# Attention and perception in one kernel: key tile 0 of half groups 5 and 15 as three one-pass products, sums by transfer for 15 of 16 half groups, and small VectorE operations joined or moved

## The chip, the cores and the metric

The kernel runs on one core of a Trainium2 chip. The metric is the device time of one launch in microseconds. A core has five engines that run their own instruction streams side by side: TensorE (PE in the profile; PEld is its weight load), VectorE (DVE), ScalarE (ACT), GpSimd (POOL) and SyncE (SP). Transfers between HBM and SBUF are started by SP, ACT and POOL.

## What is computed

Input x has 4 images of 64x64 pixels with 256 channels, all in float32. Layer 0 is full self-attention within each image, layer 1 a 3x3 depthwise "perception", a two-layer update and local attention over a 3x3 window:

```python
q, k, v = x @ Wq, x @ Wk, x @ Wv             # 32, 32 and 256 channels; 4096 pixels an image
x = gamma * softmax(q @ k.T) @ v + x
perceived = depthwise_conv3x3(x)             # 256 -> 768 channels
h = x + w_up2 @ gelu(w_up1 @ perceived)      # 768 -> 512 -> 256
q, k, v = split(h @ w_qkv)                   # 256 channels each
w = softmax over the 9 neighbours of (q . k) / 16
out = h + sum over the 9 neighbours of w * v
```

## The kernel before

**Slots and points.** The work goes through 32 slots (NSLOT); a slot is 512 queries (8 rows) of one image, eight slots make an image. Within a slot the image's 4096 keys are taken in 16 half groups, n = 0 to 15, of 256 keys, that is two key tiles of 128. A loop over 16 "points" per slot writes the instruction order by hand: each engine executes its instructions in the order in which this loop gives them. At point n stand, in this order: load_alone for half group n+1, loads of keys and values of later groups, the high parts for n+1, the energy (scores and Exp) of half group n+2, send for n+1, jobs of layer 1, product n, add_up for n+1, and some perception taps. Layer 1 follows at a distance: perception two slots behind, the hidden layer three (k = slot - 3), the local result five (a = slot - 5). A slot of attention with layer 1 beside it takes about 92.6 us.

**The product, plain and in parts.** p, the exponentials of a half group, is a 128 x 2 x 512 tile. A plain product (L481) multiplies each key tile's values (128 keys, 256 channels in two halves) with its 512 columns of p, in float32 for which TensorE makes several passes; the trace has two records for each. In parts, p is cut into high (p rounded down to the one-pass type fp32r, by ScalarE, L428 and L437), low = p - high, and gap = high - 4096 * low (VectorE, L446 and L447 for one key tile, L510 and L520 for two). Three one-pass products per channel half then stand in place of a plain one: high by v and low by a form of v go to acc banks 0 and 1, gap by another form to banks 2 and 3; evacuate joins them at the slot's end. Even half groups but 0 have both tiles in parts (IN_PARTS). Odd ones have key tile 1 in parts in "full" slots (ONE_IN_PARTS), and half groups 11 and 13 key tile 0 too (BOTH_IN_PARTS). Full slots are those with 0 < s < 31 and s > 2 that are not the last of an image: 25 of 32. alone(s, n) names the tiles that are cut one by one, load_alone loads their value forms (vo, from packed_o), high_alone and low_and_gap make the three parts. For key tile 0 of half groups 11 and 13 all four tiles stand in the "hid" buffer, which is free in the second half of a slot.

**The sums.** The softmax denominator needs the sum of p over the half groups. Those in by_dma are added by accumulating transfers that POOL issues (send, L498 and L500), even ones into one tile and odd ones into another (tags "xc" and "sent"); the rest VectorE adds (L513, L516). At n = 15 VectorE adds the two sent tiles (L528), folds (L529), and partial_sums transposes and reduces (L547, L548). A small matmul (dps, L576) and reciprocal follow in the next slot, where finish scales the result into the ring of rows xp. In full slots half groups 0 to 13 go by transfer, in the first slot of an image from 2 on; 14 and 15 are VectorE's.

**Layer 1 pieces that the change touches.** border_terms (L992, L993) forms the border pixels' key sums: one ScalarE multiply for channel half 0, one VectorE multiply-add for half 1, into edge; border then sums edge over the partitions by one matmul (L1004). local_values adds the bias to each half of a PSUM bank on VectorE (L1033). scores multiplies the local exponentials by a mask on POOL (L1086); for the first slot of an image POOL also clears rows of them (L1093, L1095). local_sum adds the pieces up on POOL (L1109, L1112, L1115). local_product scales the local result on VectorE (L1167), adds h (L1179) and has SP send it to HBM (L1180), one channel half at point 4 and one at point 5; its tiles come from the tag "o", which has two buffers and also holds the results of evacuate.

**Buffers.** tile_of(shape, tag, name, bufs) takes the next of a tag's buffers; an instruction that writes into a buffer waits until what used it before is done, a transfer's landing included. "den" has one buffer: the sum, and then the inverse of the denominator, until finish is through.

Of the kernel before, what the change touches and what calls it, by code (L numbers as in the profile page):

```python
# [9 lines left out]
F32 = mybir.dt.float32  # L10
F32R = mybir.dt.float32r
AF = mybir.ActivationFunctionType
ALU = mybir.AluOpType
AX = mybir.AxisListType
PSUM = bass.MemoryType.PSUM

P = 128
B, H, W, C = 4, 64, 64, 256
N = H * W
CQK = C // 8  # L20
CH = C // P
HP, WP = H + 2, W + 2
NB = 512
RB = NB // W
WARM = 10
NBLK = N // NB
# [10 lines left out]
NHC = HID // P  # L37
# [5 lines left out]
NSLOT = B * NBLK  # L43
# [7 lines left out]
BELOW = 1.0 - 2.0**-13  # L51
IN_PARTS = (2, 4, 6, 8, 10, 12, 14)
ONE_IN_PARTS = (1, 3, 5, 7, 9, 11, 13, 15)
BOTH_IN_PARTS = (11, 13)
BY_DMA = (3, 5, 7, 9, 11, 13)
BY_DMA_IF_FULL = tuple(range(14))


LAG_PERC, LAG_HID, LAG_ATT = 2, 3, 5
# [3 lines left out]
def attention_then_perception_kernel(  # L63
# [19 lines left out]
    nc = tc.nc  # L83
# [8 lines left out]
    ones = const.tile([P, P], F32, tag="ones", name="ones")  # L92
# [8 lines left out]
    def unshifted():  # L101
        fctx = ExitStack()
        pool = fctx.enter_context(tc.tile_pool(name="fast", bufs=1))
# [4 lines left out]
        def tile_of(shape, tag, name, bufs=1):  # L108
            return pool.tile(shape, F32, tag=tag, name=name, bufs=bufs)
# [37 lines left out]
        for r in range(4):  # L147
            nc.scalar.dma_start(
                out=bqk2[r * CQK : (r + 1) * CQK, :], in_=b_qk[:, r % 2 : r % 2 + 1]
# [17 lines left out]
        for r in range(KR):  # L167
            m = near[r * KW : (r + 1) * KW]
            for half in range(2):

                for sign in (1, -1):
                    nc.gpsimd.affine_select(
                        out=m[:, half], in_=m[:, half], compare_op=ALU.is_ge, fill=0.0,
# [20 lines left out]
        def watch(values):  # L194

            n = values.free_size()
            for i in range(0, n, P):
                at = watched[:, : min(P, n - i)]
                nc.gpsimd.tensor_tensor(at, at, values[:, i : min(n, i + P)], ALU.add)
# [22 lines left out]
        def full(s):  # L222
            return in_two_sums(s) and s > 1 and s % NBLK < NBLK - 1
# [3 lines left out]

        def alone(s, n):

            return [i for i, ns in enumerate((BOTH_IN_PARTS, ONE_IN_PARTS)) if full(s) and n in ns]  # L230

        def load_parts(to, s, which):
            pair, r = divmod(s, 2)
# [74 lines left out]
        def load_values(s, G):  # L308
            values[s, G] = tile_of([P, TPB, C], "v", f"v_{s}_{G}", 2)
            to = values[s, G].rearrange("p t c -> p (t c)")  # L310
            at = block(s, G)
            if not in_two_sums(s):
                nc.sync.dma_start(out=to, in_=packed_v[:, bass.ts(at, TPB * C)])
            elif full(s):
                nc.sync.dma_start(out=to, in_=packed_h[:, at])
            else:
                nc.sync.dma_start(out=to[:, : 2 * C], in_=packed_h[:, at, : 2 * C])
                nc.sync.dma_start(out=to[:, 2 * C :], in_=packed_v[:, bass.ts(2 * at + 1, 2 * C)])
# [8 lines left out]
        def load_alone(s, n):  # L327
            for i in alone(s, n):
                if i:
                    f, *rest = [tile_of([P, NB], "vs", f"vo_{s}_{n}", 4)] + [None] * 3  # L330
                else:
                    four = tile_of([P, NHC, NB], "hid", f"vo_{s}_{n}_0")
                    f, *rest = (four[:, j] for j in range(NHC))
                forms[s, n, i], rests[s, n, i] = f, rest
                nc.sync.dma_start(
                    out=f.rearrange("p (f c) -> p f c", c=C), in_=packed_o[:, block(s, n // 2), i]
                )
# [71 lines left out]
        sums, accs, lsums, lrdens = {}, {}, {}, {}  # L409
# [92 lines left out]
        def add_up(s, G, half):  # L502

            n = 2 * G + half
            low_and_gap(s, n)
            p = weights[s, G, half]
            if in_parts(s, G, half):
                high = highs[s, G, half]
                low, gap = (tile_of([P, 2, NB], f"p{x}", f"p{x}_{s}_{G}_{half}") for x in "lg")
                nc.vector.tensor_tensor(low.bitcast(F32R), p, high, ALU.subtract)  # L510
            if not by_dma(s, n):
                if s in sums:
                    nc.vector.tensor_tensor(sums[s], sums[s], p, ALU.add)  # L513
                elif s in firsts:
                    sums[s] = tile_of([P, 2, NB], "den", f"den_{s}")
                    nc.vector.tensor_tensor(sums[s], firsts.pop(s), p, ALU.add)  # L516
                else:
                    firsts[s] = p
            if in_parts(s, G, half):
                nc.vector.scalar_tensor_tensor(  # L520
                    gap.bitcast(F32R), low, -SPLIT, high, ALU.mult, ALU.add
                )
                lows[s, G, half], gaps[s, G, half] = low, gap
            if G == NG - 1 and half == 1:
                den = sums[s]
                for even in range(2):
                    if (s, even) in sent:
                        nc.vector.tensor_tensor(den, den, sent.pop((s, even)), ALU.add)  # L528
                nc.vector.tensor_tensor(den[:, 0, :], den[:, 0, :], den[:, 1, :], ALU.add)  # L529

        def squares(t):
            return t.rearrange("p (j r) -> p j r", r=SQ)
# [6 lines left out]
        def partial_sums(s):  # L539


            a = shared(s)
            parts_[s] = tile_of([P, 2, NJ], "parts", f"parts_{s}")
            turneds[s] = tile_of([P, CH, NB], "xc", f"turned_{s}", 2)
            todo = [sums[s][:, 0, :]] + ([] if a is None else [lsums.pop(a)])
            for i, t in enumerate(todo):
                nc.vector.transpose(turneds[s][:, i, :], t)  # L547
                nc.vector.tensor_reduce(  # L548
                    parts_[s][:, i, :], squares(turneds[s][:, i, :]), axis=AX.X, op=ALU.add
                )  # L550
            watch(parts_[s][:, : len(todo), :].rearrange("p i j -> p (i j)"))

        def on_all(values, turned, out, copy=nc.vector.tensor_copy):

# [82 lines left out]
        def late_tile(name):  # L637

            if not thirds:
                t = perc_tile(name).rearrange("p s n -> p (s n)")  # L640
                thirds[:] = [t[:, i * NB : (i + 1) * NB] for i in range(3)]
            return thirds.pop(0)
# [323 lines left out]
        def edge_row(s):  # L966
            return {0: 0, NBLK - 1: RB - 1}.get(s % NBLK)

        edge = pool.tile([P, 2 * RB + W], F32, tag="edge", name="edge")

        def border_parts(s):

# [15 lines left out]
        def border_terms(s):  # L988


            for to, of in border_parts(s):
                nc.scalar.mul(edge[:, to], of(0), wc[:, 0:1])  # L992
                nc.vector.scalar_tensor_tensor(  # L993
                    edge[:, to], of(1), wc[:, 1:2], edge[:, to], ALU.mult, ALU.add
                )

        def border(s):


            ps = job_bank(f"c_{s}")  # L1000
            row = edge_row(s)
            n_side = 2 * RB
            n = border_parts(s)[-1][0].stop
            nc.tensor.matmul(ps[0:1, :n], lhsT=ones[:, 0:1], rhs=edge[:, :n], start=True, stop=True)  # L1004
            one = pad[0:1, :]
            nc.scalar.activation(one[:, :n], ps[0:1, :n], AF.Exp, bias=bc, scale=-(C**-0.5))
            nc.gpsimd.tensor_scalar(one[:, :n], one[:, :n], 3.0, None, ALU.mult)
            if row is not None:

                ends = one[:, n_side : n : W - 1]  # L1010
                nc.gpsimd.tensor_scalar(ends, ends, 2.0 / 3.0, None, ALU.mult)
# [4 lines left out]
        def local_values(s, t):  # L1016
            ps = job_bank(f"lv_{s}_{t}")
            for half in range(2):
                for kin in range(CH):
                    nc.tensor.matmul(  # L1020
                        ps[:, half * C : (half + 1) * C],
                        lhsT=keys_of(s, t, half, kin), rhs=wlv[:, kin, :],
                        start=(kin == 0), stop=(kin == CH - 1),
                    )
            for half in range(2):
                if s < NSLOT - 2:
                    lvs[s, t, half] = tile_of([P, C], "lv", f"lv_{s}_{t}_{half}", 8)
                else:
                    if not half:
                        late[s, t] = late_tile(f"lv_{s}_{t}")  # L1030
                    lvs[s, t, half] = late[s, t][:, half * C : (half + 1) * C]
                lv = lvs[s, t, half]
                nc.vector.tensor_tensor(lv, ps[:, half * C : (half + 1) * C], blv, ALU.add)  # L1033
                if s >= NSLOT - 1:

                    square = tile_of([P, 2, NB], "den", f"lv_{s}_{t}_{half}_2")[:, 0, :C]
                    nc.gpsimd.tensor_tensor(square, lv, lv, ALU.mult)
                    watch(square)

        def pieces(s):  # L1040

# [9 lines left out]
        def scores(s, half):  # L1051
# [31 lines left out]
            mask = near[:, half, :rows, :].rearrange("p h w -> p (h w)")  # L1083
            mask = mask.unsqueeze(1).to_broadcast([P, tiles, rows * QW])
            if s < NSLOT - 2:
                nc.gpsimd.tensor_tensor(pv, pv, mask, ALU.mult)  # L1086
            else:
                nc.vector.scalar_tensor_tensor(
                    pv, pv, 1.0, mask, ALU.mult, ALU.mult, accum_out=seen()
                )  # L1090
# [735 lines left out]
```

## Time and profile before

| what | value |
|---|---|
| median of 3 runs | 3201.46 us (3201.24 to 3201.75) |
| the profiled execution's own time | 3203.15 us |
| its span, first to last instruction | 3201.4 us |
| granted TensorE clock | 0.998 |
| busy PE / DVE / ACT / POOL | 3179.4 / 2903.6 / 1550.8 / 759.6 us |
| moved by transfers | 683.26 MB, mean 213 GB/s |
| sent<-p, 512 KB, issue to landing | 6.5 us (median of 356) |
| out<-lo, 256 KB, issue to landing | 3.9 us (median of 56) |

The page gives busy time by engine, the span in 40 slices, the transfers, the chain of work that ended last, and groups of instructions with count, busy time and mean duration. The timeline lists instructions in order of time: start in us, length in us, engine, line, operation, output<-inputs, shape, count, and in brackets the idle time before it and what ended it. The windows give busy time of PE, PEld, DVE, ACT and POOL in a stretch, then clock, transfer share and GB/s. Matmul ends are modelled, so steps between starts are used for TensorE.

### The profile page before, as it was taken

The page shows a single profiled execution, that of the slowest core. Times are in us where ns is not written, and L with a number is a line of the kernel's source. Part 1 is how long each engine was busy: PE and PEld are TensorE (multiplying, and loading weights), DVE is VectorE, ACT ScalarE, POOL GpSimd, SP SyncE. Part 2 cuts the span into 40 slices and gives each one's busy share as a digit, 9 for nine tenths or more (in the row PEclk, how much of TensorE's full clock was granted, in tenths as well). Part 3 has the DMA queues.
Part 4 walks back from the last instruction along what each step waited for, and adds up shares of the span by engine and source line. Part 5 has one row for each costly group of instructions (what it writes and reads, how often), then busy time and mean ns, then how long its engine had stood idle before and what let it go on. Part 6 is the DMA issues. An engine that isn't in the chain of part 4 may idle for free.

```text
span 3201.4 us, 39239 instructions
## 1 busy us (share of the span) xinstructions
PE 3179.4 (99%) x12486; PEld 2261.7 (71%) x12486; DVE 2903.6 (91%) x4428; ACT 1550.8 (48%) x2068; POOL 759.6 (24%) x1055
## 2 busy tenths in 40 slices
PE   9999999999999999999999999999999999999998
PEld 5557777766777777776777777777677777777655
DVE  5778999998999999998999999998899999999894
ACT  4435555445545555544555545554555555455331
POOL 3201122212222221222122232211221222222121
PEclk9999999999999999999999999999999999999999
DMA  7768888777888888877878888886788888888100
GB/s 259 229 170 218 227 226 224 220 230 229 227 227 243 243 218 229 221 208 247 234 219 232 225 240 234 238 221 197 269 238 221 224 228 227 235 237 220 50 25 28
DMA packets 315588, 683.26 MB, mean 213 GB/s; under 512 B 100384, under 2 KB 101424, under 8 KB 315248
## 3 DMA queue, kind: packets, MB, share of 16 engines
q1 hardware_dynamic: 243008, 435.69, 42.6%
q0 software_dynamic: 64688, 231.54, 31.7%
q10 hardware_dynamic: 7680, 13.44, 1.1%
q8 instruction: 104, 1.70, 0.2%
q14 instruction: 108, 0.88, 0.1%
HBM read 412.46 MB, written 80.61 MB: 154 GB/s over the span
## 4 chain that ended last, share of the span: by engine, by line
PE 94%; DVE 3%; DMA 1%; issue 0%; POOL 0%; ACT 0%; SPq 0%; ACTq 0%; DVEq 0%; POOLq 0%
PE acc L481 46%; PE e L418 7%; PE dx L857 7%; PE hid_de L800 5%; PE hid_gf L800 5%; PE hid_bc L800 5%; PE lv L1020 3%; PE g L953 3%; PE lo L1154 3%; PE v L347 3%; PE s L1061 2%; PE hid_a L800 2%; DVE perc L687 1%; PE qk L272 1%; PE hid L832 1%; DMA vo<-packed_o 0%
## 5 line engine op out<-in xcount | busy, mean ns | idle before, releaser
L687 DVE SCALAR_TENSOR_TENSOR perc<-xp,wb,perc 128x526 f32<-128x526 f32 (+1 forms) x1356 | 937.7, 757 | 0.4
L423 ACT ACTIVATE p<-e 128x1024 f32<-128x1024 f32 x512 | 524.9, 1025 | 485.9 <-PE e L418 409.4
L481 PE MATMUL acc<-p,v 128*128 128x512 f32 x1472 | 678.9, 596 | 0.2 <-ACT v L363 0.2
L500 POOL DMA_DIRECT2D sent<-p x304 | 258.0, 855 | 1353.6 <-ACT p L423 823.0
L481 PEld LDWEIGHTS acc<-p,v 128*128 128x128 f32 x1472 | 275.1, 190 | 267.9 <-issue 257.6
L418 PE MATMUL e<-qa,ka 128*128 128x512 f32 x1024 | 357.1, 430 | 5.3 <-ACT p L423 1.5
L428 ACT ACTIVATE ph<-p 128x1024 fp32r<-128x1024 f32 x203 | 215.1, 1060 | 198.4 <-PE acc L481 134.7
L510 DVE TENSOR_TENSOR pl<-p,ph 128x1024 fp32r<-128x1024 f32 x203 | 256.1, 1262 | 16.8 <-ACT ph L428 16.8
L481 PE MATMUL acc<-ph,v 128*128 128x512 f32 x812 | 264.3, 447 | 0.2
L520 DVE SCALAR_TENSOR_TENSOR pg<-pl,ph 128x1024 fp32r<-128x1024 f32 x203 | 253.3, 1248 | 11.9 <-DVE pl L510 0.5
L418 PEld LDWEIGHTS e<-qa,ka 128*128 128x128 f32 x1024 | 190.9, 188 | 86.0 <-issue 39.9
L437 ACT ACTIVATE oh<-p 128x512 fp32r<-128x512 f32 x200 | 126.4, 632 | 248.4 <-PE acc L481 83.2
L857 PE MATMUL dx<-hid,wup 128*128 128x512 f32 x512 | 229.8, 592 | 0.0
L481 PE MATMUL acc<-pl,vf 128*128 128x512 f32 x812 | 223.3, 397 | 0.0
L481 PE MATMUL acc<-pg,vf 128*128 128x512 f32 x812 | 219.1, 391 | 2.0 <-DVE pg L520 2.0
L481 PEld LDWEIGHTS acc<-ph,v 128*128 128x128 f32 x812 | 148.2, 189 | 51.9 <-issue 26.8
L481 PE MATMUL acc<-oh,v 128*128 128x512 f32 x400 | 184.8, 543 | 0.0
L481 PEld LDWEIGHTS acc<-pg,vf 128*128 128x128 f32 x812 | 152.3, 188 | 39.1 <-DVE pg L520 3.3
L481 PEld LDWEIGHTS acc<-pl,vf 128*128 128x128 f32 x812 | 152.7, 188 | 37.1
L823 ACT ACTIVATE hid<-hid,bup 128x512 f32<-128x512 f32 x120 | 80.3, 716 | 199.1 <-DVE hid L807 199.1
L693 DVE TENSOR_TENSOR perc<-perc 128x262 f32<-128x262 f32 x360 | 170.8, 488 | 6.3
L857 PEld LDWEIGHTS dx<-hid,wup 128*128 128x128 f32 x512 | 96.7, 189 | 98.5 <-issue 93.4
(231 smaller groups left out, 5476.1 us busy)
## 6 DMA issues: line engine op xcount, KB each, us to landing
sent<-p POOLq DMA_DIRECT2D x356, 512.0 KB, 6.5
vf<-packed_f SPq DMA_DIRECT2D x203, 512.0 KB, 5.7
v<-packed_h SPq DMA_DIRECT2D x200, 512.0 KB, 4.7
ka<-packed SPq DMA_DIRECT2D x1016, 64.0 KB, 3.3
vo<-packed_o SPq DMA_DIRECT2D x250, 256.0 KB, 3.9
xp<-in_x SPq DMA_DIRECT2D x30, 528.0 KB, 6.9
packed_f<-vlg POOLq DMA_DIRECT2D x28, 512.0 KB, 4.3
xc<-in_x SPq DMA_DIRECT2D x56, 256.0 KB, 4.3
```

The lines of the kernel that those rows point to most:

```text
L418: nc.tensor.matmul(e[:, i, :], lhsT=keys[s, G][:, bass.ts(2 * half + i, P)].bitcast(F32R), rhs=queries[s].bitcast(F32R), start=True, stop= ...
L423: nc.scalar.activation(p, e, AF.Exp)
L428: nc.scalar.activation(high.bitcast(F32R), weights[s, G, half], AF.Identity, scale=BELOW)
L437: nc.scalar.activation(high.bitcast(F32R), p, AF.Identity, scale=BELOW)
L481: nc.tensor.matmul(accs[s][to + c], lhsT=w[:, bass.ts(c, P)].bitcast(kind), rhs=x.bitcast(kind), start=to not in started[s], stop=last,)
L500: nc.gpsimd.dma_start(out=sent[s, even], in_=p, accum_op=ALU.add)
L510: nc.vector.tensor_tensor(low.bitcast(F32R), p, high, ALU.subtract)
L520: nc.vector.scalar_tensor_tensor(gap.bitcast(F32R), low, -SPLIT, high, ALU.mult, ALU.add)
L687: nc.vector.scalar_tensor_tensor(acc, win, wt, acc, ALU.mult, ALU.add)
L693: nc.vector.tensor_tensor(t[:, to, :], t[:, a, :], t[:, b, :], op)
L800: nc.tensor.matmul(ps[:, n * C : (n + 1) * C], lhsT=w(j), rhs=rows_of(mixes[s, j][:, kind, :]), start=(j == 0), stop=(j == MULT - 1),)
L857: nc.tensor.matmul(ps, lhsT=wup2[:, d, bass.ts(c, P)], rhs=hids[s][:, d, :], start=(d == 0), stop=(d == NHC - 1),)
```

## The change

Key tile 0 of half groups 5 and 15 joins the tiles in parts (5 not in the first slot of an image, where v's plain tile is loaded over the high one). For 15 its four tiles stand in "hid", as for 11 and 13; for 5 the value form and the high part stand in "den", low and gap in the two buffers of "o". Half group 14 is summed by transfer too, so only 15 is left to VectorE, which starts the sum from the even sent tile. partial_sums reduces both transposed tiles in one operation. The border's second channel half is multiplied on ScalarE and added by a second matmul. local_values adds the bias in one operation of 512 columns. The masks go from POOL to VectorE.

```diff
-BOTH_IN_PARTS = (11, 13)
+BOTH_IN_PARTS = (5, 11, 13, 15)
-BY_DMA_IF_FULL = tuple(range(14))
+BY_DMA_IF_FULL = tuple(range(15))
...
         def alone(s, n):
-            return [i for i, ns in enumerate((BOTH_IN_PARTS, ONE_IN_PARTS)) if full(s) and n in ns]
+            if not full(s) or n not in ONE_IN_PARTS:
+                return []
+            return [0, 1] if n in BOTH_IN_PARTS and (n > NHC * 2 or s % NBLK) else [1]
...
                 nc.sync.dma_start(out=to, in_=packed_h[:, at])
+                n = 2 * G + 1
+                if n in BOTH_IN_PARTS and 0 not in alone(s, n):
+                    nc.sync.dma_start(
+                        out=to[:, 2 * C : 3 * C],
+                        in_=packed_v[:, (2 * at + 1) * 2 * C : (2 * at + 1) * 2 * C + C],
+                    )
...
                     f, *rest = [tile_of([P, NB], "vs", f"vo_{s}_{n}", 4)] + [None] * 3
-                else:
+                elif n > NHC * 2:
                     four = tile_of([P, NHC, NB], "hid", f"vo_{s}_{n}_0")
                     f, *rest = (four[:, j] for j in range(NHC))
+                else:
+                    two = tile_of([P, 2, NB], "den", f"vo_{s}_{n}_0")
+                    f, *rest = two[:, 0], two[:, 1], *(
+                        tile_of([P, NB], "o", f"o{x}_{s}_{n}_0", 2) for x in "lg"
+                    )
...
                     nc.vector.tensor_tensor(sums[s], sums[s], p, ALU.add)
-                elif s in firsts:
+                elif n == 0:
+                    firsts[s] = p
+                else:
+                    first = firsts.pop(s) if s in firsts else sent.pop((s, 1))
                     sums[s] = tile_of([P, 2, NB], "den", f"den_{s}")
-                    nc.vector.tensor_tensor(sums[s], firsts.pop(s), p, ALU.add)
-                else:
-                    firsts[s] = p
+                    nc.vector.tensor_tensor(sums[s], first, p, ALU.add)
...
             for i, t in enumerate(todo):
                 nc.vector.transpose(turneds[s][:, i, :], t)
-                nc.vector.tensor_reduce(
-                    parts_[s][:, i, :], squares(turneds[s][:, i, :]), axis=AX.X, op=ALU.add
-                )
-            watch(parts_[s][:, : len(todo), :].rearrange("p i j -> p (i j)"))
+            parts = parts_[s][:, : len(todo), :].rearrange("p i j -> p (i j)")
+            turned = turneds[s][:, : len(todo), :].rearrange("p i n -> p (i n)")
+            nc.vector.tensor_reduce(parts, squares(turned), axis=AX.X, op=ALU.add)
+            watch(parts)
...
             for to, of in border_parts(s):
-                nc.scalar.mul(edge[:, to], of(0), wc[:, 0:1])
-                nc.vector.scalar_tensor_tensor(
-                    edge[:, to], of(1), wc[:, 1:2], edge[:, to], ALU.mult, ALU.add
-                )
+                for c in range(CH):
+                    nc.scalar.mul(edge[:, c, to], of(c), wc[:, c : c + 1])
...
-            nc.tensor.matmul(ps[0:1, :n], lhsT=ones[:, 0:1], rhs=edge[:, :n], start=True, stop=True)
+            for c in range(CH):
+                nc.tensor.matmul(
+                    ps[0:1, :n], lhsT=ones[:, 0:1], rhs=edge[:, c, :n],
+                    start=(c == 0), stop=(c == CH - 1),
+                )
...
-                nc.vector.tensor_tensor(lv, ps[:, half * C : (half + 1) * C], blv, ALU.add)
...
+            bias = blv.unsqueeze(1).to_broadcast([P, 2, C])
+            nc.vector.tensor_tensor(lv, ps.rearrange("p (a c) -> p a c", a=2), bias, ALU.add)
...
             if s < NSLOT - 2:
-                nc.gpsimd.tensor_tensor(pv, pv, mask, ALU.mult)
+                nc.vector.tensor_tensor(pv, pv, mask, ALU.mult)
```

The value projection splits a block's key tile 0 as well for the two half groups (the branch "both" of project_v), eight blocks in all.

More of the change, by code (lines that the diff above doesn't have):

```diff
@@ L967, in edge_row @@
             return {0: 0, NBLK - 1: RB - 1}.get(s % NBLK)
-        edge = pool.tile([P, 2 * RB + W], F32, tag="edge", name="edge")
+        edge = pool.tile([P, CH, 2 * RB + W], F32, tag="edge", name="edge")
         def border_parts(s):
@@ L1024, in local_values @@
                     )
+            if s < NSLOT - 2:
+                lv = tile_of([P, 2, C], "lv", f"lv_{s}_{t}", 4)
+            else:
+                lv = late_tile(f"lv_{s}_{t}").rearrange("p (a c) -> p a c", a=2)
             for half in range(2):
[L1026 to L1032, printed above, removed]
-                nc.vector.tensor_tensor(lv, ps[:, half * C : (half + 1) * C], blv, ALU.add)
[L1034 to L1038, printed above, removed]
+                lvs[s, t, half] = lv[:, half]
+            bias = blv.unsqueeze(1).to_broadcast([P, 2, C])
+            nc.vector.tensor_tensor(lv, ps.rearrange("p (a c) -> p a c", a=2), bias, ALU.add)
+            if s >= NSLOT - 1:
+                square = tile_of([P, 2, NB], "den", f"lv_{s}_{t}_2")[:, 0, :]
+                nc.gpsimd.tensor_tensor(square.rearrange("p (a c) -> p a c", a=2), lv, lv, ALU.mult)
+                watch(square)
         def pieces(s):
```

## The prediction

> **What bounds the kernel now.** I read the page first, then busy time in stretches of 100 us, then one slot (1018 to 1110 us, slot 11) as VectorE's timeline, TensorE's chain of waits and SyncE's transfers.
>
> ```profile
> PE 3179.4 (99%) x12486; PEld 2261.7 (71%) x12486; DVE 2903.6 (91%) x4428; ACT 1550.8 (48%) x2068; POOL 759.6 (24%) x1055
> ...
> PE 94%; DVE 3%; DMA 1%; issue 0%; POOL 0%; ACT 0%; SPq 0%; ACTq 0%; DVEq 0%; POOLq 0%
> ```
>
> TensorE (PE) is never without work, so only fewer passes on it make the kernel shorter. But VectorE (DVE) is full beside it wherever attention and perception run together:
>
> ```profile
> 1000.00:1100.00 100.00, 100.00 (x412) 74.82 (x411) 96.08 (x144) 52.65 (x70) 27.02 (x33) 1.00 0.86 235
> 1100.00:1200.00 100.00, 100.00 (x410) 74.35 (x409) 96.22 (x140) 50.34 (x65) 31.67 (x40) 1.00 0.84 229
> ```
>
> The third busy number is DVE's: 96%, and most of the rest is a few hundredths between instructions. In slot 11, 92.8 us long, its idle pieces over 0.1 us add up to 2.1 us, 1.6 of them just after the slot's start. So there are two clocks, and a delay of DVE of over some 2 us in one place reaches TensorE. The place that matters is half group 5, where a local result is written out:
>
> ```profile
> 1054.96 0.69 DVE L1167 SCALAR_TENSOR_TENSOR lo<-lo,lrden 128x512 f32<-128x512 f32 x1 [0.16 <-PE lo L1154]
> ...
> 1055.69 0.69 DVE L1179 TENSOR_TENSOR lo<-lo,h 128x512 f32<-128x512 f32 x1
> 1056.30 0.68 DVE L446 TENSOR_TENSOR ol<-p,oh 128x512 fp32r<-128x512 f32 x1
> 1057.02 0.69 DVE L447 SCALAR_TENSOR_TENSOR og<-ol,oh 128x512 fp32r<-128x512 f32 x1
> 1057.63 4.82 DVE L687 SCALAR_TENSOR_TENSOR perc<-xp,wb,perc 128x526 f32<-128x526 f32 x7
> 1062.37 0.68 DVE L1167 SCALAR_TENSOR_TENSOR lo<-lo,lrden 128x512 f32<-128x512 f32 x1
> ...
> 1063.70 1.22 DVE L510 TENSOR_TENSOR pl<-p,ph 128x1024 fp32r<-128x1024 f32 x1
> 1064.95 1.22 DVE L520 SCALAR_TENSOR_TENSOR pg<-pl,ph 128x1024 fp32r<-128x1024 f32 x1
> ```
>
> ```profile
> 1058.18 1.54 PE lo L1154 x12
> 1059.72 3.12 PE acc L481 x10
> ...
> 1063.31 3.43 PE dx L857 x8
> 1066.74 2.78 PE acc L481 x12
> ```
>
> ```profile
> 1056.41 0.36 SPq L1180 DMA_DIRECT2D out<-lo  x1
> ```
>
> ```profile
> DMA to landing us min/median/max: 6.8/6.8/6.8
> ```
>
> The last two are the transfer of that result to HBM: issued at 1056.41, 0.03 us after the add of L1179 ends, landed 6.8 us later. Read for the 20 slots spoken of below (5, 6, 9 to 14, 17 to 22, 25 to 30), it takes 5.4 to 6.8 us in 19 and 2.8 in one, mean 5.76. It is the first of a slot's two that is so slow; the second mostly takes 2.2 to 4.
>
> [...] The trace's fastest out<-lo takes 2.0 us[...]. [...] at 1099.20 a gap of 128x512 takes 1.34 us beside POOL's mask at 1098.77 where 0.69 is usual; set against the same operations elsewhere, each mask operation lengthens DVE's work by about 0.8 us. [...]
>
> **The change part by part.** DVE's costs are steps from start to start in slot 11.
>
> Half groups 5 and 15 in parts: the chain gives 3.11 us for a half group with one key tile in parts and 2.74 with both (pieces of 12 at 1008.51 and 1093.54 us), so 0.37 saved each. 15 occurs in the 25 full slots, 5 in the 22 of them that do not begin an image: 47 x 0.37 = 17.4 us less on TensorE. Each costs ScalarE 0.63 (at 48%, hidden), a load of 256 KB issued before its use (its buffers are free early), and DVE 2 x 0.67 = 1.33 us.
>
> The border's second matmul: 0.13 us for 16 columns and 0.23 for 80, so 24 x 0.13 + 8 x 0.23 = 5 us more on TensorE; DVE loses 2 x 0.17 us per slot. Net on TensorE -12.4 us, all the change can gain.
>
> DVE per slot: +2.67 (two tiles), -1.25 (one add of 1024 fewer, since 14 goes by transfer), -0.33 (border), -0.1 (two joined bias adds), -0.15 (joined reduce), +2 x 0.5 for the masks ([...] 0.43 from the step of 262 columns; 0.5 taken), -2 x 0.8 for POOL's masks that no longer block it: about +0.2. For the idle 1.9 us that is harmless. Bounds -0.6 and +1.8 (no relief at all) hardly exceed the cover.
>
> Eight value blocks that are split on both tiles instead of one cost DVE 0.7 us each where it idles 14 us per slot or, in the first image, more: nothing. The second load for half group 5 in slots 8, 16, 24 waits on SyncE for the first, some 4.7 us, behind which are loads made three half groups ahead: nothing; without that cover, at most 4.7 x 3.
>
> **The wait that is added.** New low and gap for key tile 0 of half group 5 stand in the "o" tiles, two buffers, taken at point 4 (ahead of half group 5) just before local_product takes the same two for its results. The built program puts the gap (og_5_0) and the first result (lo_0) at the same address, and before that gap, on DVE, stands a wait for the completion of out<-lo of the same slot, in exactly these 20 slots. DVE writes lo_0 (L1179), then the new low, then must stand until the transfer that it has just caused has landed. Behind it are the old low and gap of 5, seven taps, the second result, low and gap of 6.
>
> In slot 11's times, with the mean landing: result ready 1056.38, new low to 1057.1, landing 1056.41 + 5.76 = 1062.17, new gap done about 1063.0: DVE stands 5.1 us. TensorE begins half group 5 at 1059.72 and wants this gap after four of twelve matmuls, 1060.63: it waits 2.4, and ends at 1064.85 instead of 1062.85. DVE then does the old pair (to 1064.3), taps (4.74, to 1069.05), the result (1.33), low of 6 (to 1071.6), gap (1072.85). TensorE would be at 1064.85 + 0.46 + 3.43 = 1068.74 for half group 6, after the highs at 1069.67: it waits 2.0 for low and 0.3 for gap and ends at 1073.8 against 1069.52: +4.28. DVE is then 6.7 late, 2.4 more than TensorE; half groups 8 and 10 leave 2.7 and 3 us, g at 1076.98 only 2.3, so 0.2 more. Less 0.37 for half group 15, plus 0.13 for the border: +4.25 per slot, 20 x 4.25 = 85 us. DVE comes level again in the 1.6 us it used to idle at the slot's start.
>
> The sum by transfer: half group 14's goes out on POOL behind the local sum (six adds of 0.97, 1.1 for the sides, 1.26 more with an edge row), and the final sum on DVE now waits for it. Mostly the local sum starts earlier than before, since the masks are off POOL, and ends some 2 us after the second mask: send at about 1107.6, landed 7 later (half group 13's take 7.4 to 7.6 there), DVE arriving at 1113.2 in shifted time, 1.5 us of standing, against 2.4 us that the evacuation of acc has to spare: 0.3 per slot, 5 us. But in slots 11, 19, 27 POOL clears the image's top rows in the masks' tiles (L1093, L1095), which must wait for the second mask on DVE; the whole local sum, 9.2 us, comes after. Send 1114.7, landed 1121.5, evacuation done about 1128.4 where TensorE is ready at 1121.75: 6.6 x 3 = 20 us.
>
> Slots 3, 4, 8, 16, 24 have no such wait: -2 us; borders elsewhere +1. Sum: 85 + 5 + 20 - 2 + 1 = +109; I take 103, since transfers have a little more time per byte in longer slots. The profiled execution took 3203.15 us (span 3201.4), 1.7 above the median of the runs, 3201.46, which I ignore. 3203 + 103 = 3306.
>
> **Rivals.** Shorter landing: if out<-lo lands in 4.2 us (its queue emptier, since vo leaves earlier), each slot gives back 1.56: 20 x 2.7 = 54, and the final sum's wait falls to 10: 3266. For it: one slot had 2.8; against: 19 had over 5.3.
> Longer: landing in 7 us, and the final sum standing in all slots: 20 x 5.5 + 52 = +162, 3365.
> Faster, by one mechanism: the wait for out<-lo is covered. Low and gap of half group 6 are ready 2.0 to 2.4 us before TensorE wants them in the shortened slot; of it 1.33 goes to the new pair, leaving about 0.9, and 0.6 per slot is gained elsewhere. It turns to gain when landing takes under about 2.3 us. Then -17.4 + 5 = -12.4: 3191. Against it: only one of twenty is near. A wait that isn't carried out as built would end here too.
> Nothing measurable: landing near 2.4 us, 3201.
>
> **How the numbers follow.** Main case, 3306 (3270 to 3345 by landings of 4.8 to 6.8): 0.62. Shorter: 0.15. Longer: 0.11. Faster: 0.09. No change: 0.03. The range leaves out faster and no change and half of the tails: 3245 to 3360. A measurement of this kernel tells about 0.2% from no change; faster by more 0.09, within 0.03, slower by more 0.88.
>
> **What would show it.** Right (lines of the changed kernel): DVE idle about 5 us before a gap (L462) in 20 slots, ended by DMA out<-lo; TensorE idle 2 to 2.5 before og of half group 5 and again before pl of 6; slots of about 97 us; in three slots a den wait (L534) of 7 us. Masks on DVE of 0.57 us, and gaps beside POOL near 0.7. Wrong: slots under 93 us, the landing of out<-lo under 2.5 us, or idle TensorE in other half groups.

## The result, and the profile after

| | before | after |
|---|---|---|
| median | 3201.61 us (6 runs, 3200.35 to 3203.56) | 3348.28 us (6 runs, 3340.59 to 3353.3) |
| ratio | | 1.0449, 95% interval 1.0438 to 1.0461 |
| profiled execution, span | 3203.15, 3201.4 | 3348.92, 3347.2 |
| granted TensorE clock | 0.998 | 0.986 |

The change costs 147 us; the forecast was 103 (3306 us, range 3245 to 3360). The page of the kernel after gives busy time (share, instructions) and the chain of work that ended last:

```profile
PE 3222.7 (96%) x12644; PEld 2294.6 (69%) x12644; DVE 2907.0 (87%) x4385; ACT 1586.8 (47%) x2195; POOL 669.6 (20%) x1017
...
PE 70%; DVE 16%; DMA 9%; issue 3%; SPq 1%; POOL 1%; ACT 1%; ACTq 0%; DVEq 0%; POOLq 0%
```

TensorE held 94% of the chain and has 70% now; VectorE and transfers have most of the rest. VectorE does no more than it did (2907 us against 2904), but is busy for less of the time. The two stretches of 100 us that were shown of before (the third busy number is VectorE's, the fraction after POOL's is the granted clock):

```profile
1000.00:1100.00 100.00, 96.53 (x389) 71.06 (x388) 90.66 (x136) 50.28 (x71) 19.73 (x27) 0.98 0.84 225
1100.00:1200.00 100.00, 88.68 (x360) 67.18 (x359) 81.12 (x121) 46.86 (x66) 20.96 (x32) 0.95 0.79 212
```

Half group 5 on VectorE, in slot 10:

```profile
981.41 0.69 DVE L1184 SCALAR_TENSOR_TENSOR lo<-lo,lrden 128x512 f32<-128x512 f32 x1 [0.15 <-PE lo L1171]
...
982.15 0.69 DVE L1196 TENSOR_TENSOR lo<-lo,h 128x512 f32<-128x512 f32 x1
982.75 0.69 DVE L461 TENSOR_TENSOR ol<-p,vo 128x512 fp32r<-128x512 f32 x1
989.08 0.69 DVE L462 SCALAR_TENSOR_TENSOR og<-ol,vo 128x512 fp32r<-128x512 f32 x1 [5.64 <-DMA out<-lo]
989.69 0.68 DVE L461 TENSOR_TENSOR ol<-p,oh 128x512 fp32r<-128x512 f32 x1
990.41 0.69 DVE L462 SCALAR_TENSOR_TENSOR og<-ol,oh 128x512 fp32r<-128x512 f32 x1
991.02 4.82 DVE L703 SCALAR_TENSOR_TENSOR perc<-xp,wb,perc 128x526 f32<-128x526 f32 x7
995.76 0.68 DVE L1184 SCALAR_TENSOR_TENSOR lo<-lo,lrden 128x512 f32<-128x512 f32 x1
```

The bracket is the idle time before the instruction and what ended it: 5.64 us, and everything under that line comes later by it. TensorE in the same piece:

```profile
986.51 0.63 PE L496 MATMUL acc<-ol,vo 128*128 128x512 f32 x2
989.83 0.74 PE L496 MATMUL acc<-og,vo 128*128 128x512 f32 x2 [2.68 <-DVE og L462]
...
992.25 3.60 PE L873 MATMUL dx<-hid,wup 128*128 128x512 f32 x8
995.28 1.49 PE L496 MATMUL acc<-ph,v 128*128 128x512 f32 x4
998.37 1.19 PE L496 MATMUL acc<-pl,vf 128*128 128x512 f32 x4 [1.59 <-DVE pl L525]
```

Two stands (idle time in which the engine waits), 2.68 and 1.59. Over the run, from the lists of waits (sum in us, how often, the longest):

```profile
DVE og L462 <- DMA out<-lo: 107.9, 20, 6.9
```

```profile
PE acc L496 <- DVE og L462: 51.4, 17, 4.0
PE e L433 <- ACT p L438: 24.5, 4, 8.2
PE acc L496 <- DVE pl L525: 8.1, 7, 1.6
PE acc L496 <- DMA vo<-packed_o: 4.8, 10, 1.0
```

**Slot by slot.** Take the time between two folds of the sum on VectorE (L529 before, L545 after) as a slot's length, and split it into what VectorE works and what it idles in pieces over 0.11 us. Of the 20 slots with the new wait, 11, 19 and 27 differ and stand apart.

| mean per slot, us | before | after | measured | forecast |
|---|---|---|---|---|
| 17 slots: length | 92.45 | 98.34 | +5.89 | +4.25 |
| VectorE at work | 90.35 | 90.62 | +0.27 | +0.2 |
| VectorE idle | 2.10 | 7.72 | +5.62 | +4.05 |
| slots 11, 19, 27: length | 92.76 | 107.90 | +15.14 | +10.85 |
| the 11 other lengths, sum | 1121.0 | 1119.8 | -1.2 | about -1 |

17 x 5.89 + 3 x 15.14 - 1.2 = 144.3, nearly all of the 145.8 by which the span grew. The miss lies in 17 x 1.64 = 28 and 3 x 4.3 = 13 us.

**The three slots.** The end of slot 11: POOL, and what waits for it.

```profile
1129.97 0.18 POOL L1110 MEMSET lp<- 64x99 f32 x1 [1.61 <-DVE lp L1103]
...
1130.93 5.96 POOL L1126 TENSOR_TENSOR lsum<-lsum,lp 128x99 f32<-128x99 f32 x6
...
1138.21 0.59 POOL L515 DMA_DIRECT2D sent<-p  x1
```

```profile
1147.63 1.02 ACT L438 ACTIVATE p<-e 128x1024 f32<-128x1024 f32 x1 [9.02 <-DMA sent<-p]
```

```profile
1148.71 1.22 PE L433 MATMUL e<-qa,ka 128*128 128x512 f32 x2 [7.93 <-ACT p L438]
```

POOL clears rows after the second mask, adds up, and only then sends half group 14, which takes 9.4 us to land. Until then its p can't be overwritten: ScalarE stands, the energy banks stay full, and TensorE stands 7.93 us. VectorE stands beside it (8.74 us before the final sum).

### The profile page after: what moved, and what is told of

It reads as the page before. It is cut to its first block, busy times and chain, and to the rows that moved or that the text cites. A ratio compares the mean times of both kernels' runs of the same rounds, so it can differ in the third digit from the quotient of the medians.

```text
span 3347.2 us, 39766 instructions
## 1 busy us (share of the span) xinstructions
PE 3222.7 (96%) x12644; PEld 2294.6 (69%) x12644; DVE 2907.0 (87%) x4385; ACT 1586.8 (47%) x2195; POOL 669.6 (20%) x1017
## 4 chain that ended last, share of the span: by engine, by line
PE 70%; DVE 16%; DMA 9%; issue 3%; SPq 1%; POOL 1%; ACT 1%; ACTq 0%; DVEq 0%; POOLq 0%
PE acc L496 32%; DVE perc L703 6%; PE e L433 5%; PE hid_bc L816 5%; PE hid_gf L816 5%; PE hid_de L816 5%; PE dx L873 4%; DMA out<-lo 4%; PE lv L1038 3%; PE v L362 3%; PE g L969 2%; PE hid_a L816 2%; DMA vo<-packed_o 2%; PE lo L1171 2%; DVE pl L525 2%
## 5 line engine op out<-in xcount | busy, mean ns | idle before, releaser
L496 PE MATMUL acc<-p,v 128*128 128x512 f32 x1284 | 590.0, 596 | 0.2 <-ACT v L378 0.2
L515 POOL DMA_DIRECT2D sent<-p x329 | 272.2, 833 | 1536.7 <-ACT p L438 1044.7
L496 PEld LDWEIGHTS acc<-p,v 128*128 128x128 f32 x1284 | 241.0, 190 | 243.0 <-issue 234.8
L496 PE MATMUL acc<-og,vo 128*128 128x512 f32 x444 | 147.6, 415 | 51.4 <-DVE og L462 51.4
L496 PE MATMUL acc<-oh,v 128*128 128x512 f32 x400 | 170.1, 507 | 0.0
```

Source lines behind the costliest of these rows:

```text
L496: nc.tensor.matmul(accs[s][to + c], lhsT=w[:, bass.ts(c, P)].bitcast(kind), rhs=x.bitcast(kind), start=to not in started[s], stop=last,)
L515: nc.gpsimd.dma_start(out=sent[s, even], in_=p, accum_op=ALU.add)
```

## The experiments

In three of them VectorE's stand before the gap (the wait theory) is taken away in different manners; two take away the late send; two fill TensorE's idle; five look for what is left. All stand against runs of the kernel before on the same chip, 3203 to 3205 us. Kernels with zero-weight matmuls add only zeros to acc; none leaves work out.

**Without half group 5.**

```diff
-BOTH_IN_PARTS = (5, 11, 13, 15)
+BOTH_IN_PARTS = (11, 13, 15)
```

> Key tile 0 of half group 5 goes back to a plain product; all else as changed. If the wait of the new gap for out<-lo is the cause, its 20 slots lose about 5.9 us each (the slots of about 98.5 us come back to about 92.6): near 3226 us, of which some 27 us over the kernel before are the late final sum in slots 11, 19 and 27. If it is VectorE's added work (1.33 us a slot for this tile) that counts and not the wait, only 20 to 30 us go: near 3320 us. If the final sum is the bulk, it stays above 3300 us.

3237.24 us, ratio 1.0103 (1.0086 to 1.0120), 11 us above what the wait theory gave. Half group 5's tile alone costs 111 us where it should save TensorE 8.

**The same work, another buffer.** Low and gap of half group 5 in one tile of tag xc instead of two of tag o; nothing else differs.

```diff
-                    f, *rest = two[:, 0], two[:, 1], *(
-                        tile_of([P, NB], "o", f"o{x}_{s}_{n}_0", 2) for x in "lg"
-                    )
+                    lg = tile_of([P, 2, NB], "xc", f"olg_{s}_{n}_0", 2)
+                    f, *rest = two[:, 0], two[:, 1], lg[:, 0], lg[:, 1]
```

> Half group 5 stays in parts with the same instructions, but low and gap of its key tile 0 stand in a buffer of tag xc instead of the two of tag o, so the gap waits for no transfer. Wait theory: VectorE's idle 5.4 us before that gap is gone, about 3203 - 12 + 27 = 3218 us. Work theory (VectorE overloaded by the added pair): the time stays near 3340 us, since no instruction is gone.

3245.46 us, 1.0126 (1.0109 to 1.0142). VectorE's work in a slot is 90.71 (90.62 with tag o), its idle 2.49 instead of 7.72: 103 of the 147 us go with the wait for out<-lo, though no instruction is gone. The sum's stand in slots 11, 19, 27 remains (103.3 us long). The time is still 27 us above the 3218 that the wait theory gave; what these are is found below.

**The rows cleared on VectorE.** The memsets L1110 and L1112 on nc.vector, so that POOL has none of them between the masks and the send.

> As changed, but the image's top rows in the masked exponentials are cleared by VectorE instead of POOL, so in slots 11, 19 and 27 the local sum need not start after the second mask. If POOL's order makes half group 14's transfer late there, these three slots come from about 107.9 to about 98.9 us: near 3321 us. If the final sum is late only because VectorE itself is late, less than 8 us change: above 3340 us.

3327.46 us, 1.0385 (1.0368 to 1.0403): 20.8 us back. The three slots are 99.7 long now, 8.2 less in each, and still 1.1 longer than the others of this kernel (98.6).

**Half group 14 back in VectorE's sum.**

```diff
-BY_DMA_IF_FULL = tuple(range(15))
+BY_DMA_IF_FULL = tuple(range(14))
```

> The changed kernel with half group 14 back in VectorE's sum, as before; the wait of the gap for out<-lo stays. Late-send theory (slots 11, 19, 27 are 10 to 11 us longer than their neighbours since half group 14's transfer leaves behind POOL's late local sum): these three slots become as long as the others, 98 us, and the time falls to 3315 to 3325. Rival (VectorE's work, which this raises by 1.25 us in 25 slots, sets the length of a slot): 3345 to 3375.

3317.50 us, 1.0361 (1.0346 to 1.0377): 30.8 us back. Slots 11, 19, 27 are 98.5 long, as the others (98.2). VectorE works 0.85 longer in each of the 17 slots (91.47), and they are no longer for it: the wait has the slack.

**Both mended: tag xc and the rows on VectorE.**

> Both mends together: low and gap in tag xc, rows cleared by VectorE. If the two waits are all that the change lost and the rest gains 12.4 us of TensorE as summed: near 3192 us, faster than the kernel before. If VectorE at 96% can't carry the added pairs and masks: 3203 us or more, with TensorE idle before low and gap of half groups 12 to 15.

3224.07 us, 1.0063 (1.0037 to 1.0090). Neither of the two great stands is left; still it is 21 us slower than before, 32 over what was expected. The ordinary slots are 93.18 long.

**Is it the clock?** After most of its long stands in the changed kernel (14 of the 17 before og) TensorE gets half its clock (0.50 granted). Its clock record has 19 such stretches between slot 2 and the last, 82 us long in all; the kernel before has none there. Slot 11 in pieces of 4 us:

```profile
1084.00:1088.00 4.00, 1.11 (x6) 0.58 (x4) 0.46 (x1) 0.00 (x0) 0.80 (x1) 0.99 1.01 232
1088.00:1092.00 4.00, 3.71 (x10) 3.00 (x11) 3.96 (x7) 0.63 (x1) 0.00 (x0) 0.58 0.46 95
1092.00:1096.00 4.00, 4.00 (x13) 1.95 (x12) 3.97 (x8) 1.32 (x2) 0.84 (x1) 1.00 0.26 50
```

0.58 granted, just after the stand. 82 us at half clock are up to 41 us of work lost, just the size of the miss (3348 - 3306 = 42). So the stand was filled with matmuls by zero weights, 9 before og of half group 5 and 8 before pl of half group 6:

```diff
+            idle = {}
+            if full(s) and s % NBLK and s >= LAG_ATT and n in (5, 6):
+                idle = {5: {2: 9}, 6: {2: 8}}[n]
             for k, (w, to, x, kind) in enumerate(todo):
+                for _ in range(idle.get(k, 0)):
+                    nc.tensor.matmul(
+                        accs[s][0], lhsT=zeros.bitcast(F32R), rhs=todo[0][2].bitcast(F32R),
+                        start=False, stop=False,
+                    )
```

> The changed kernel with one-pass matmuls whose weights are zero put where TensorE stands: 9 before og of key tile 0 in half group 5 and 8 before pl of half group 6, in the 20 slots that wait for out<-lo. They add nothing to the result; each takes some 0.23 us, so 17 x 0.23 = 3.9 us per slot of work that mostly lies in idle time of 2.5 and 1.6 us. Clock theory (the lowered clock after TensorE stands is the term of some 40 us that the sum lacked): the stretches at half clock in the middle of the run mostly go, the granted clock is 0.995 or more, and the time falls to 3315 to 3335 although TensorE has more to do. Rival (the clock has nothing to do with the standing, or the lost time lies elsewhere): the stretches stay, and the time is 3348 or up to 20 us above it.

3346.46 us, 1.0448 (1.0433 to 1.0463), clock 0.994. No stretch at half clock is left in half groups 5 and 6, as the clock theory had it, and the time is the same, as the rival had it. That can be read in two ways, since the second filling took 1.87 us of TensorE, more than the stand of 0.46 it was put in. So the first alone, with 8:

> The changed kernel with 8 zero-weight one-pass matmuls ahead of og of key tile 0 in half group 5 alone, about 2.0 us where TensorE stands 2.4 us on average; none before pl of half group 6, where the 8 of the earlier run took 1.87 us of TensorE's path and so can have hidden what the full clock gave back. Clock theory (the half clock after the stand costs TensorE some 1.5 us a slot, which ends on the path): the stretches at half clock in half group 5 are gone and the time falls to 3310 to 3335. Rival (VectorE's wait for out<-lo alone sets the slot, the clock only fills TensorE's slack): 3342 to 3352.

3351.25 us, 1.0463 (1.0447 to 1.0479), clock 0.993. Slot 10 of this kernel:

```profile
988.64 2.02 PE L500 MATMUL acc<-vo,zeros 128*128 128x512 f32 x8
991.57 0.73 PE L506 MATMUL acc<-og,vo 128*128 128x512 f32 x2 [0.90 <-DVE og L464]
...
1000.11 1.20 PE L506 MATMUL acc<-pl,vf 128*128 128x512 f32 x4 [1.58 <-DVE pl L535]
```

The rival holds. With its full clock, TensorE stands 1.4 us per slot before pl of half group 6, where it stood 0.46: what it gained in speed it waits. The changed kernel shows it by itself. In the 14 slots with a stretch at half clock in half group 5, the stand before pl is 0 to 0.2; in 9, 10 and 26, where the clock stayed full after 2.83, 2.68 and 2.48 us of standing, it is 1.57 to 1.59. From the start of VectorE's late gap (og) to the first matmul of g (a job of layer 1 at point 8) it is 19.02 to 19.08 us in all 17 ordinary slots, with the stretch or without it; only slot 27, with two stretches one after the other, has 19.59. Half clock filled a wait that was there anyway. Where none is left to fill, it costs: in the kernel with 8 fillings three slots (13, 14, 27) got their stretch behind the stand before pl, and there the same distance is 20.62, 1.6 us more.

**What the 21 us are.** Cut TensorE's time at the first of each pair of energy matmuls. A slot then falls into 16 pieces, each with the product of one half group (the energies run two half groups ahead) and the jobs of layer 1 beside it. Mean change against the kernel before, over the 17 slots:

| piece with the product of half group, us | forecast for after | after | tag xc, rows on VectorE | also 14 on VectorE | also masks and rows on POOL |
|---|---|---|---|---|---|
| 5 and 6 | +4.28 | +4.41 | -0.31 | -0.31 | -0.31 |
| 13 | 0 | +0.80 | +0.99 | +0.89 | +0.13 |
| 14 (with the border) | +0.13 | +0.03 | +0.04 | +0.08 | +0.89 |
| 15 | -0.37 | -0.04 | +0.03 | -0.38 | -0.38 |
| all 16 pieces | +4.25 | +5.42 | +0.77 | +0.51 | +0.39 |

The kernel with both mends loses at half group 13, whose tiles the change leaves as they were, and gains nothing at 15. Over the 25 full slots these are 21.7 us, and 0.9 in place of 25 x -0.37 = -9: nearly all of the 32. (In the forecast 0.2 lies at g, which has no row.) The loss at 13 is there with the stands of half groups 5 and 6 and without them. It was looked for with half group 14 on VectorE,

> Low and gap in one tile of tag xc and the rows cleared on VectorE, as in the run that gave 3224, and half group 14 back in VectorE's sum: one transfer of 512 KB per slot less, one add of 1.22 us on VectorE more. Transfer theory (the 21 us that were left come from value forms that land late behind more traffic, and from the final sum's wait): 3203 to 3214. Rival (VectorE's work is what was left): 25 x 1.25 = 31 us more, 3235 to 3255.

3218.47 us, 1.0050 (1.0037 to 1.0063): between both theories, nearer the first. Half group 15 now has its gain (its load lands after 2.7 us on average instead of 5.0), and 13 still loses. VectorE works 91.55 in a slot and idles 1.46 (90.70 and 2.48 without); slots 93.00. Then also with the masks and the clearing back on POOL:

> Low and gap in one tile of tag xc, half group 14 in VectorE's sum, and the masks and the clearing of rows back on POOL: what is left of the change is both key tiles in parts for 5 and 15, the joined operations and the border. Mask theory (masks of 0.94 on VectorE cost it 1.9 us per slot, more than POOL's masks took from it): faster than the same with masks on VectorE by 10 to 25 us, 3188 to 3200. Rival (POOL's masks delay VectorE by 0.8 each as they did before, so the move is even or a gain): the same within 6 us or slower, 3205 to 3225.

3222.67 us, 1.0059 (1.0046 to 1.0072). The rival is right: masks on VectorE are even or a small gain. But the reason for 3222 is another than above. VectorE works 92.21 and idles 0.96, and nearly all the slots are within 0.1 of 93.17: here VectorE is the bound. TensorE waits for it at half group 14 (+0.89) and hardly loses at 13 (+0.13). Moving the masks gives VectorE 92.21 - 91.55 = 0.66 us a slot.

Then half group 13's four tiles in den and o, so that its load need not wait until half group 11 is done with hid (first slots of an image left as they were):

```diff
-                elif n > NHC * 2:
+                elif n in (11, 15) or n == 13 and not s % NBLK:
...
+                        lg = [tile_of([P, NB], "o", f"o{x}_{s}_{n}_0", 2) for x in "lg"]
```

> As the run with low and gap of half group 5 in tag xc and the rows cleared on VectorE (3224), but the four tiles of key tile 0 of half group 13 stand in den and o instead of hid, in all full slots but the first of an image: their load no longer waits for half group 11's product, nor half group 15's for 13's. Landing theory (TensorE stands 0.8 us a slot before a value form that was asked for too late, since one buffer serves 11, 13 and 15): these stands go and the time falls to 3195 to 3210, perhaps below the kernel before. Rival (the queue's traffic makes them late wherever they stand, or the stand moves to another wait): 3216 to 3228.

3217.62 us, 1.0034 (1.0021 to 1.0048), as the rival had it. The stand before key tile 0 of half group 13 is gone and stands before key tile 1, 0.77 us a slot: its load leaves no earlier (77.1 us after the fold in slot 11) and takes 8.6 us to land. Last, half group 15 plain, with 14 by transfer and on VectorE:

```diff
-BOTH_IN_PARTS = (5, 11, 13, 15)
+BOTH_IN_PARTS = (5, 11, 13)
```

> As the run that gave 3224 (low and gap of half group 5 in tag xc, rows cleared on VectorE), without half group 15's key tile 0 in parts: one load of 256 KB at the slot's end and one use of hid less, two VectorE operations of 0.67 us less, 0.37 us more on TensorE. Landing theory (the 1.2 us that a slot loses between the scores and the next local values come from value forms that land late at the slot's end, with half group 15's load and half group 14's transfer among the causes): the loss falls by half or more, 3203 to 3213. Rival (the loss is there without it, from half group 14's transfer alone): TensorE has 25 x 0.37 = 9 us more to do, 3225 to 3235.

> The same with half group 14 back in VectorE's sum, so that the slot's end has the transfers of the kernel before; left of the change are half group 5's key tile 0 in parts, the masks, the joined operations and the border. VectorE should need about 91.5 - 1.3 = 90.2 us and its fixed 0.9 of idle, below TensorE's 92.2. Landing theory: slots as long as TensorE's work, 3190 to 3202, with at most 8 us to gain from half group 5. Rival (the loss stands at the slot's end for another reason, such as the masks having left POOL, whose sends now start earlier): 3207 to 3220.

3222.89 (1.0056, 1.0043 to 1.0070), 2 us below the rival's range, and 3220.62 us (1.0050, 1.0036 to 1.0064), 1 us above it: in both the landing theory was wrong. The second has the transfers of the kernel before at the slot's end, and half group 13's piece is 1.04 longer in it (0.81 in the first). So neither half group 15's load nor half group 14's transfer is needed for that loss. The rival named in the last, the sends, is seen when the queues are laid side by side. Half group 13's two loads and its send, slot 10 before, SyncE and then POOL:

```profile
1002.19 0.81 SPq L335 DMA_DIRECT2D vo<-packed_o  x2
```

```profile
1001.36 0.96 POOL L1086 TENSOR_TENSOR lp<-lp,near 128x396 f32<-128x396 f32 x1 [4.73 <-ACT lp L1081]
1002.27 0.86 POOL L500 DMA_DIRECT2D sent<-p  x1
```

The mask holds the send back until the first load has left. In the kernel with tag xc and the rows on VectorE, slot 10, SyncE, POOL, and TensorE after:

```profile
1004.98 0.85 SPq L349 DMA_DIRECT2D vo<-packed_o  x2
```

```profile
1004.03 0.84 POOL L514 DMA_DIRECT2D sent<-p  x1 [2.48 <-DMA sent<-p]
1004.56 0.84 POOL L1121 MEMSET lsum<- 128x512 f32 x1
```

```profile
1013.14 1.17 PE L495 MATMUL acc<-vo 128*128 128x512 f32 x4 [1.39 <-DMA vo<-packed_o]
```

No mask, the send of 512 KB leaves first, and TensorE waits for the load. Means over the 17 slots (send and load from the fold, in us), and in the last two rows over slots 11, 19 and 27:

| kernel | masks | send of 13 | first load of 13 | it lands after | 13's piece |
|---|---|---|---|---|---|
| before | POOL | 77.31 | 77.19 | 3.98 | |
| xc, 14 on VectorE, masks on POOL | POOL | 76.00 | 75.43 | 4.39 | +0.13 |
| after | VectorE | 80.38 | 81.83 | 7.08 | +0.80 |
| xc, rows on VectorE | VectorE | 75.60 | 77.02 | 7.49 | +0.99 |
| the same, 15 plain, 14 on VectorE | VectorE | 76.00 | 77.43 | 7.45 | +1.04 |
| after, slots 11, 19, 27 | VectorE | 85.51 | 82.72 | 3.83 | +0.01 |
| after with the rows on VectorE, slots 11, 19, 27 | VectorE | 81.45 | 82.41 | 8.04 | +1.23 |

The order of the third to fifth rows holds in eight more of the kernels with masks on VectorE: the send is 1.4 us ahead on average, ahead in every one of the 17 slots, and the load lands after 7.0 to 7.6 us.

The last two rows differ by the engine of four short memsets alone, and by the order that follows from it. In slots 11, 19 and 27 of the changed kernel POOL's clearing waits for VectorE's mask, and so does the send behind it, while the load doesn't. Slot 11, SyncE and POOL:

```profile
1124.74 0.87 SPq L350 DMA_DIRECT2D vo<-packed_o  x2
```

```profile
1127.26 0.18 POOL L1112 MEMSET lp<- 64x99 f32 x1
1127.52 0.84 POOL L515 DMA_DIRECT2D sent<-p  x1
```

The load leads there, lands early, and TensorE loses nothing at half group 13. With the clearing on VectorE and nothing else changed, the send leads in these slots too, and TensorE loses 1.23. The other kernels agree: in the 18 such slots of the six with masks on VectorE and clearing on POOL the piece is at most 0.03 longer, in the 15 of the five with both on VectorE (that with 13's tiles moved left out) 0.56 to 1.46 longer. And the landing is what TensorE waits for: it begins the low part of 13's key tile 0 some 0.13 us after it in 11 to 20 of the 20 slots of the eleven kernels with masks on VectorE and 13's tiles in hid, in 1 of the kernel before and in none with the masks on POOL.

To leave ahead of its own send is not enough: with half group 13's tiles in den and o the load left 1.2 us ahead of it but 3.7 behind the send of 12 (6.4 before), and landed after 9.7 us. By what way a send already under way makes the load late was not shown; measured against the kernel before, the load with the send ahead of it landed 3.1 to 3.5 us later.

## Why the prediction was right in kind and short in size

**The wait.** Right in place, number and size: 20 stands of 5.4 us on average (forecast 5.1), landing after 5.88 us (5.76), 103 us by experiment. TensorE in half groups 5 and 6: +4.41 us (forecast +4.28). That the means agree so well is in part luck: in slots 13, 18 and 25 the result landed in 2.4 to 2.9 us, in the other 17 in 5.7 to 7.4. A send of 512 KB had left 0.57 us ahead of it in those 17, and 0.32 ahead or 0.30 behind in the three; v of 512 KB had left 1.8 to 2.2 ahead in all 20. In the 17 TensorE stood 2.2 to 4.0 before og of half group 5, and where its clock stayed full 1.6 before pl of 6; where it didn't, the half clock took the place of the second stand.

**"DVE comes level again in the 1.6 us it used to idle at the slot's start": this step failed.** In the 17 slots VectorE's stand was 5.19 us, but the rest of its idle time, which the sum had shrink by 1.05 us, grew by 0.43. That is 1.48 x 17 = 25 of the 41 us missed. VectorE idles there mostly for TensorE, before lv and hid (0.97 and 1.47 us a slot, against 0.86 and 1.03 before the change), so it can catch up only if TensorE is not late itself. And TensorE lost at the slot's end: from the pieces of 13 to 15 it was to take 0.24 less, and it took 0.79 more.

**"A load of 256 KB issued before its use (its buffers are free early)" was true of half group 5 alone.** Half group 15's load leaves late, since hid is handed from 11 to 13 to 15, and beside half group 14's transfer it lands late too (5.0 us with tag xc and the rows on VectorE, 2.7 without that transfer): of the 0.37 to be saved 0.04 came. Half group 13's load was not in the sum at all. Before, it had its 4 us of landing because a mask kept POOL's send behind it. The masks were costed by what they add to VectorE and take from it (0.66 us a slot gained, 0.6 forecast), and not by what follows them on POOL. That the order makes the load late and TensorE wait is shown by slots 11, 19 and 27 of two kernels. What the masks alone would cost the kernel before isn't shown: it wasn't run with only its masks moved.

**The late send.** The three slots were right, the way was not, and the size was too small: it is not the evacuation that comes late but the p tiles, whose reuse waits for the landing. In the profile the three slots are 9.6 us longer than the ordinary ones, not 6.6: TensorE stands 7.9 us before an energy matmul in slot 11 (8.2 and 7.3 in 19 and 27), and half clock of 6.8 to 10.2 us begins in that stand, with 3.6 to 4.7 of it behind the stand's end. The rows on VectorE gave back 20.8 us, half group 14 on VectorE 30.8 (20 forecast). Counted whole, the three slots make 13 of the 41 us missed, with the 25 above 38.

**The range of the main case.** 3270 to 3345 for landings of 4.8 to 6.8 us does not follow from the sum, which changes by 20 us for 1 us of landing and gives 3287 to 3327. 3348 lies above both, within the whole range of 3245 to 3360.

**TensorE's saving.** Forecast 0.61 per slot with both tiles. Where nothing waits, half group 5 gave 0.31 and 15 gave 0.38, and the border's second matmul took 0.06 a slot: 0.63.

**VectorE's sum** of +0.2 was +0.27. The mask of 0.57 is 0.55 to 0.57 us where POOL is still, and up to 0.97 where POOL adds beside it; its mean is 0.71. On POOL, before, a mask lengthened VectorE's operations beside it by 0.63 us on average (0.8 taken).

The half clock looked like the missing term, by its size, and wasn't: behind the stand of half group 5 it costs nothing (19.02 to 19.08 us with a stretch and without). Behind the late sends it wasn't taken away by itself. The rival "longer" (3365) came nearer in time by a wrong reason: neither did landings take 7 us nor did the final sum stand in all slots.

## What to carry to other kernels

Before tiles are put into a buffer "that is free", follow its ring one full turn: the last user may be a transfer that the same engine has started a microsecond ago, and its landing then stands in the middle of that engine's queue (here VectorE stood 5.4 us on average, 20 times). An operation moved off a queue moves what is queued behind it: in the kernels with the masks on VectorE the send of 512 KB left 1.4 us ahead of the load instead of 0.1 behind it, and the load landed 3.1 to 3.5 us later. A cost that equals the gap in the sum is no evidence until a run takes it away: from the end of VectorE's wait on, slots with one stretch at half clock and without took the same time within 0.06 us, since another wait was there to be filled.

## What was not expected of the hardware

- Half clock (0.50 granted) came in stretches of 3.41 us, or two or three of them in a row (6.83 and 10.24 us). Of the 17 stands before og, of 2.24 to 3.96 us, 14 had one, which began between 0.94 us before the stand's end and 1.27 after it; those of 2.48, 2.68 and 2.83 us had none.
- Matmuls by zero weights (0.25 us each) in the stand before og: with 9 of them, and 8 before pl, none of the 20 slots had a stretch in half groups 5 and 6; with 8, and none before pl, one had it in 5 and three after the stand of 1.6 before pl.
- Landings of the same 256 KB: 4.0 us with the send of 512 KB issued 0.1 us behind the load, 3.8 with it 2.8 behind, 7.0 to 7.6 with it 1.4 us ahead.
